# Moving side work to other steps in an attention and conv kernel: first chunks, fetches, reciprocals, last k and v, a band

## The chip, the cores and the metric

The kernel runs on one core of a Trainium2 chip. The metric is the device time of one execution in microseconds (us). TensorE (PE) multiplies, ScalarE (ACT) and VectorE (DVE) work elementwise, GpSimd (POOL) issues the accumulating DMAs and does small things, SyncE (SP) issues most of the other DMAs. Each engine works through its own instructions in order, and an instruction waits until what it needs is there.

## The reference

The input x is 4 images of 128 channels and 64 x 64 pixels, float32. Two layers follow each other. The first is attention with a residual:

```python
x_norm = _group_norm(x, norm_w, norm_b)              # 8 groups of 16 channels
qkv = jnp.einsum('oc,bchw->bohw', qkv_w, x_norm) + qkv_b[None, :, None, None]
q, k, v = jnp.split(qkv, 3, axis=1)                  # 4 heads of 32 channels, 4096 positions
attn = jax.nn.softmax(jnp.einsum('bhid,bhjd->bhij', q, k) * scale, axis=-1)
out = jnp.einsum('bhij,bhjd->bhid', attn, v)
return x + proj(out)
```

The second is a block of two 3x3 convolutions with quantized weights (3 bits), each followed by a batch norm over all four images, and a residual:

```python
out = jax.nn.relu(batchnorm(conv3x3(x, lsq_quantize(w1, alpha1))))
out = batchnorm(conv3x3(out, lsq_quantize(w2, alpha2)))
return jax.nn.relu(out + x)
```

## The kernel before

**Attention.** The queries of each image are cut into 8 blocks of 512 (`blocks`, 32 in all, numbered n; b is the image and qb the block in it). A block goes over the 4096 keys in 32 steps of 128, called kt. A step has two pairs of heads: `scores` (line 442) multiplies q and k for one pair into PSUM and ScalarE takes the exponential (`p`, line 444). `weights` (line 456) multiplies `p` with v into `acc`, in two halves of 256 queries each. The sum over keys is kept elementwise in `r` by VectorE (lines 469 and 471), except for the steps in `MOVED` = 4, 9, 14, 19, 24, 28, whose `p` tiles are summed into `rm` by accumulating DMAs of 1 MB each on GpSimd's queue (lines 464 and 466). `merge` (line 492) adds `rm` to `r` by another one at the start of the next block. There are 9 buffers for `p` tiles, 9 for k, 9 for v, 2 for q and 3 for x chunks.

**The order.** The order is written out by hand. The loop takes three pairs of scores, then three halves of weights, and so on, so TensorE goes in groups: 12 score matmuls, 24 value matmuls. After each half the function `side` emits what is due. `schedule(n, before)` makes this list for block n: `add(kt, f)` puts f after step kt, `at_half(p, f)` after half p, and `visit(i, first, second, evacuate)` puts matmuls of a projection at the end of the i-th group (`ends[i]`), both parts in one place if `split` is False, and the copy out of PSUM one half later. A place in this list is a place in each engine's order; it isn't a time.

**What is at its side.** After a block its result is finished during the next one: `sums` multiplies `r` by ones (`l`, line 488), `spread` stores the sums in another layout (`lq`, line 523), `invert` takes the reciprocals and stores them to DRAM (`rd`, line 529), `gather` reads them back spread over 128 partitions (`rc`, line 534), `weigh` multiplies (`av`, line 537), `residual` loads the x chunk, `project` and `store` end it (`po`, `y<-x`). `project_parts` gives the chunks: 512 columns of k, q or v, each 16 or 32 small matmuls (line 317) and copies on ScalarE and VectorE (lines 351, 352, 371); the chunks k and q go to DRAM (`kd`, `qd`) and come back by `load_k` and `load_q` in another layout. The norm of the next image is done by `late[b]`, of which entry 8 computes v's bias `bvn`. `pieces` are small steps of the quantization of the conv weights.

**The start.** The x chunks of image 0 are loaded, `keep_warm` issues matmuls that nobody reads, the statistics are taken (`mv`, `gm`), and the first chunks of k, q and v are projected before the first scores. The other chunks of image 0 lie in block 0, and the queries of blocks 2 to 7 in block 1.

**The conv.** A band is 18 rows of the padded image; `load_band` reads it from DRAM (line 582), `split_band` parts it in a high and a low half (`hi`, `lo`, lines 573 and 574), `conv` multiplies both (line 781). `layer` goes through the 16 bands and calls `prepare(m)` (here `first`) after band m. The first bands are loaded in the last attention block.

The loads and stores on SyncE's queue all stand in one order, and when one waits, those behind it wait too.

Of the kernel before, what the change touches and what calls it, by code (L numbers as in the profile page):

```python
# [78 lines left out]
def _fast_body(ctx, tc, x, norm_w, norm_b, qkv_wt, qkv_b, proj_wt, proj_b,  # L79
               w1, alpha1, gamma1, beta1, w2, alpha2, gamma2, beta2, out, cnt):  # L80
    nc = tc.nc
# [4 lines left out]
    NB = N // FB  # L86
# [53 lines left out]
    wqd = dram.tile([P, TAPS, P], F32, name="wqd")  # L140
# [80 lines left out]
    sums = att.enter_context(tc.tile_pool(name="sums", bufs=2))  # L221
# [84 lines left out]
    def keep_warm(count):  # L306

        t = psa.tile([P, FB], F32, name=f"idle{count}", tag="a")
        for _ in range(count):
            nc.tensor.matmul(t[:, 0:P], gavg, gavg, start=True, stop=True)  # L310
# [95 lines left out]
    def load_k(b, j):  # L406
        k = k_tile(b, j)
        for s in range(4):
            i, part = divmod(s, 2)
            src = kd[b, j][part].rearrange("(g i d) n -> i d g n", i=2, d=D)  # L410
            nc.sync.dma_start(out=f32(k)[s * D : (s + 1) * D, :, :], in_=src[i])
# [5 lines left out]
    def load_q(b, j):  # L417
        q = q_tile(b, j)
        src = qd[b, j].rearrange("s (g i d) n -> i g d s n", i=2, d=D)
        for s in range(4):  # L420
            for g in range(2):
                nc.sync.dma_start(out=f32(q)[s * D : (s + 1) * D, g, :, :], in_=src[s // 2, g])
# [161 lines left out]
    def split_band(b, g):  # L584
        ready[0, b, g] = split(raw[b, g], f"0_{b}_{g}")
# [5 lines left out]
        eng.dma_start(out=halves[j // 4][:, j % 4, :], in_=x_chunk(0, j))  # L591
    table = const.tile([P, 1], F32, name="table")
    nc.scalar.activation(table, mhalf, AF.Exp)
    keep_warm(26)
    st = small.tile([P, NB, 6], F32, name="st0", tag="st")
    for j in range(NB):
        nc.vector.bn_stats(st[:, j, :], halves[j // 4][:, j % 4, :])
# [14 lines left out]
    def load_kv(b, j):  # L612
        load_k(b, j)
        load_v(b, j)

    for what, j in (("k", 0), ("q", 0), ("k", 1), ("v", 0), ("k", 2), ("v", 1), ("k", 3), ("v", 2),
                    ("v", 3)):
        for f in first_chunk(j, what, True):
            f()
        if what == "q":  # L620
            five_v()
            six_v()
        if what == "v" and j < 3:
            load_k(0, j + 1)


# [3 lines left out]
    def fetch(b, j):  # L630
        xin[b, j] = load_x(b, j)

    def schedule(n, before):
        b, qb = blocks[n]
        todo = []
        ends = [p for p in range(2 * NK - 2) if (2 * n * NK + p) % 3 == 2]
        two = b + 1 < B and qb in ((3, 4, 5) if b == 0 else (2, 3))

        def at_half(p, f):
            todo.append((p, f))  # L640

        def add(kt, f):
            todo.append((2 * kt + 1, f))

        def visit(i, first, second, evacuate=None, split=True):
            at_half(ends[i], first)
            e = ends[i + 1 if split else i]
            at_half(e, second)  # L650
            if evacuate:
                at_half(e + 1, evacuate)
            return e

        if before:
            add(1, before["merge"])
            e = visit(5 if two else 4 if n == 1 else 6, lambda: before["sums"](0), lambda: before["sums"](1),
                      split=not two and n != 1)
            at_half(e + 2, before["spread"])
            at_half(e + 6, before["invert"])  # L660
            at_half(e + 8, before["gather"])
            at_half(e + 12, before["residual"])
            at_half(ends[18] - 4, before["weigh"])
            at_half(ends[18], before["project"])
            at_half(ends[18] + 2, before["store"])
        if n + 1 < len(blocks):
            add(24 if n == 0 else 14, lambda: load_q(*blocks[n + 1]))
        if n == 0:
            for i, what, j in ((0, "k", 4), (2, "k", 5), (4, "v", 4), (6, "k", 6), (8, "v", 5),
                               (10, "k", 7), (12, "q", 1), (14, "v", 6), (16, "v", 7)):  # L670
                visit(i, *first_chunk(j, what, False), split=False)
                if what == "k":
                    at_half(ends[i] + 5, lambda j=j: load_k(0, j))
        if n == 0:
            for j in (2, 3):
                add(25 + j, lambda j=j: fetch(0, j))
        if n == 1:
            for i, j in zip((0, 2, 8, 10, 12, 14), range(2, NB)):
                if j > 3:
                    at_half(ends[i - 3], lambda j=j: fetch(0, j))  # L680
                visit(i, *project_parts(0, j, lambda j=j: xin[0, j])["q"], split=False)
        qn = qb if b else qb - 1
        if b + 1 < B:
            if qn == 1:
                st = small.tile([P, NB, 6], F32, name=f"st{b + 1}", tag="st")
                for j in range(NB):
                    add(3 * j // 2, lambda j=j: fetch(b + 1, j))
                    add(3 * j // 2 + 3, lambda j=j: nc.vector.bn_stats(st[:, j, :], xin[b + 1, j]))
                late[b] = norm_parts(b + 1, st)
                add(15, late[b][0])  # L690
                for i in (0, 1):
                    at_half(ends[13 + 2 * i], late[b][1 + 2 * i])
                    at_half(ends[13 + 2 * i] + 3, late[b][2 + 2 * i])
            if qn == 2:
                at_half(ends[1], late[b][5])
                at_half(ends[1] + 1, late[b][6])
                at_half(ends[1] + 1, late[b][7])
                at_half(ends[1] + 4, late[b][8])
            if b == 0:
                chunks = {2: (), 3: (0, 1), 4: (2, 3), 5: (4, 5), 6: (6,), 7: (7,)}  # L700
            else:
                chunks = {1: (), 2: (0, 1), 3: (2, 3), 4: (4,), 5: (5,), 6: (6,), 7: (7,)}
            for i, j in enumerate(chunks.get(qb, ())):
                p = project_parts(b + 1, j, lambda j=j: xin[b + 1, j])
                if not two:
                    for what, i in dict(k=1, q=10, v=13).items():
                        visit(i, *p[what])
                    continue
                for what, e in (dict(k=2, q=7, v=9) if i == 0 else dict(k=11, q=13, v=15)).items():
                    visit(e, *p[what], split=False)  # L710
                if i == 1:
                    add(8, lambda j=j: fetch(b + 1, j))
            if qn > 0 and qb + 1 in chunks:
                add(22, lambda j=chunks[qb + 1][0]: fetch(b + 1, j))
            if qb == NB - 1:
                for j in range(NB - 1):
                    add(4 * j + 1, lambda j=j: load_kv(b + 1, j))
        if b > 0 and qb == 0:
            add(1, lambda: load_kv(b, NB - 1))


        if b == B - 1 and qb < NB - 1:
            for kt in (1, 10, 20):
                add(kt, lambda: next(pieces, None))
        elif 0 < b and qb == 0:
            for kt in (1, 10, 15, 20, 25) + ((29,) if b == 1 else ()):
                add(kt, lambda: next(pieces))
        if n == len(blocks) - 1:
            add(5, lambda: load_band(0, 0))
            add(13, lambda: split_band(0, 0))  # L730
            add(17, lambda: load_band(0, 1))
            add(24, lambda: split_band(0, 1))
            add(27, lambda: load_band(0, 2))
        return sorted(todo, key=lambda t: t[0])
# [58 lines left out]
    last["residual"]()  # L793
    conv(ready[0, 0, 0], early[0][:, 1, :], 1, wq[0])
    split_band(*bandlist[2])
    last["sums_at_once"]()
    conv(ready[0, 0, 1], early[1][:, 0, :], 0, wq[0])
    conv(ready[0, 0, 1], early[1][:, 1, :], 1, wq[0])
# [6 lines left out]
    cv = [mid.tile([P, N], F32, name=f"cv{b}") for b in range(B)]  # L805
    raw_w = mid.tile([P, TAPS, P], F32, name="raw_w")
    wq.append(mid.tile([P, TAPS, P], F32R, name="wq1"))
    nc.sync.dma_start(out=raw_w, in_=wqd)


    a_q, a_g, a_n = ([small.tile([P, 1], F32, name=f"{n}{i}") for i in range(2)]
# [50 lines left out]
    def count_bad():  # L862

        big = small.tile([P, 1], F32, name="big")
        nc.vector.tensor_reduce(big, worst, AX.X, ALU.max)
        bad = small.tile([P, 1], F32, name="bad")
        nc.vector.tensor_scalar(bad, big, LIMIT, None, ALU.is_gt)
        nbad = psa.tile([P, FB], F32, name="nbad", tag="a")
        nc.tensor.matmul(nbad[0:1, 0:1], bad, ones[:, 0:1], start=True, stop=True)
        nc.vector.tensor_copy(cnt, nbad[0:1, 0:1])  # L870

    def first(m):
        if m == 5:
            count_bad()
        if m == 6:
            nc.vector.tensor_copy(wq[1], raw_w)
        if m + 3 < len(bandlist):
            load_band(*bandlist[m + 3])
        if m + 2 < len(bandlist) and m > 0:
            split_band(*bandlist[m + 2])  # L880
# [527 lines left out]
```

## Time and profile before

| | |
|---|---|
| time, median of 3 runs | 2569.15 us (2565.08 to 2569.88) |
| span of the profiled execution | 2567.4 us |
| TensorE busy | 2515.2 us |
| VectorE busy | 2137.1 us |
| ScalarE busy | 2086.7 us |
| GpSimd busy | 282.9 us |
| DMA, mean | 157 GB/s |
| blocks of attention, from the first copy of `acc` to the last | 108.6 to 2250.8 us |
| granted TensorE clock, mean | 0.992 |

Busy times overlap, as the engines work at the same time. In the profile's rows a number such as L442 is the line of the kernel; `s<-q,k` is what it writes and reads, with buffer numbers left out. In a timeline a row has the start, the length, the engine, the line, the operation and its count, and in brackets the idle time ahead of it and what ended it. In the waits a row has the total, the number of times and the longest. SPq is SyncE's queue of DMA issues. PE counts as busy while a matmul is in it, so it says nothing about how well the array is filled.

### The profile page before, as it was taken

Reading aid. Unit: us, or ns where it says so; the run is one execution under the profiler, and the core shown is the slowest. Engines: PE = TensorE matmul, PEld = TensorE weight load, DVE = VectorE, ACT = ScalarE, POOL = GpSimd, SP = SyncE. Lnnn points to the kernel's source line nnn. Section 1 sums busy time; section 2 is a strip of 40 time slices with the busy share of each in tenths; the row PEclk is TensorE's granted clock in tenths of the full one; section 3 lists DMA queues with packets and bytes.
Section 4 is the critical chain, followed back from the end, with each engine's and each line's share of the span. In section 5 each row is a group of like instructions: output and inputs, shape, how many; then the busy total and the mean of one; then the engine's idle time right before and its main releaser. Section 6 shows DMA issues by size and latency. Waiting matters only on the chain.

```text
span 2567.4 us, 65010 instructions
## 1 busy us (share of the span) xinstructions
PE 2515.2 (98%) x28696; PEld 1504.3 (59%) x28696; DVE 2137.1 (83%) x1402; ACT 2086.7 (81%) x2278; POOL 282.9 (11%) x462
## 2 busy tenths in 40 slices
PE   8999999999999999999999999999999999999995
PEld 6555555555555555555555555555555555567774
DVE  5889888889988898889988988889999999954345
ACT  5889888998988899999988999989999999911224
POOL 2111111111011111110111111111000011000000
PEclk9999999999999999999999999999999999999997
DMA  6777667688766776797767667896666667645004
GB/s 179 179 187 164 171 176 180 158 202 188 176 151 174 169 167 155 167 222 172 169 167 175 154 154 165 194 202 149 148 137 143 145 147 149 143 87 162 1 1 165
DMA packets 148825, 403.85 MB, mean 157 GB/s; under 512 B 59416, under 2 KB 60184, under 8 KB 119992
## 3 DMA queue, kind: packets, MB, share of 16 engines
q0 software_dynamic: 45984, 280.92, 47.8%
q1 hardware_dynamic: 100680, 113.07, 17.3%
q10 hardware_dynamic: 1872, 5.64, 0.6%
q8 instruction: 227, 3.72, 0.6%
q14 instruction: 62, 0.51, 0.1%
HBM read 107.48 MB, written 56.42 MB: 64 GB/s over the span
## 4 chain that ended last, share of the span: by engine, by line
PE 85%; DMA 6%; issue 4%; DVE 3%; ACT 1%; SPq 0%; POOL 0%; ACTq 0%; POOLq 0%; DVEq 0%
PE s L442 38%; PE acc L456 34%; PE c L781 8%; DMA rm<-p 3%; DVE r L471 2%; PE pk L317 1%; PE l L488 1%; PE po L317 1%; PE pq L317 1%; PE pv L317 1%; DMA t<-y 1%; ACT p L444 1%; DMA rd<-rq 0%; ACT res L946 0%; DMA x<-in_x_dram 0%
## 5 line engine op out<-in xcount | busy, mean ns | idle before, releaser
L444 ACT ACTIVATE p<-s 128x1024 f32<-128x1024 f32 x2048 | 1949.6, 1032 | 216.0 <-PE s L442 161.4
L471 DVE TENSOR_TENSOR r<-r,p 128x2048 f32<-128x2048 f32 x768 | 1758.2, 2289 | 69.4 <-ACT p L444 18.7
L442 PE MATMUL s<-q,k 64*128 64x512 f32 x8192 | 1140.6, 409 | 6.7 <-ACT p L444 5.5
L456 PE MATMUL acc<-p,v 128*32 128x256 f32 x16384 | 1027.1, 383 | 1.0 <-DVE v L371 1.0
L442 PEld LDWEIGHTS s<-q,k 64*128 64x128 f32 x8192 | 715.1, 185 | 417.4 <-issue 167.7
L456 PEld LDWEIGHTS acc<-p,v 128*32 128x32 f32 x16384 | 462.6, 109 | 485.6 <-issue 249.2
L466 POOL DMA_DIRECT2D rm<-p x160 | 139.1, 870 | 848.0 <-ACT p L444 602.7
L848 ACT COPY cv<-c 128x512 f32<-128x512 f32 x60 | 35.2, 587 | 204.1 <-DVE st L847 204.1
L781 PE MATMUL c<-hi,wq 128*128 128x512 f32 x540 | 140.4, 404 | 3.8 <-DVE hi L573 2.5
L781 PE MATMUL c<-lo,wq 128*128 128x512 f32 x540 | 138.6, 401 | 0.0
L847 DVE BATCH_NORM_STATS2 st<-c 128x6 f32<-128x512 f32 x60 | 41.9, 699 | 103.1 <-PE c L781 82.8
L781 PEld LDWEIGHTS c<-hi,wq 128*128 128x128 f32 x540 | 102.2, 190 | 33.4 <-issue 5.0
L781 PEld LDWEIGHTS c<-lo,wq 128*128 128x128 f32 x540 | 101.6, 188 | 27.2
L352 DVE SCALAR_TENSOR_TENSOR kst<-pk,b,kst 128x512 fp32r<-128x512 f32 x32 | 24.0, 750 | 81.3 <-PE s L442 54.9
L469 DVE TENSOR_TENSOR r<-p,p 128x2048 f32<-128x2048 f32 x32 | 73.2, 2288 | 14.9 <-ACT p L444 14.9
L352 DVE SCALAR_TENSOR_TENSOR qst<-pq,b,qst 128x512 fp32r<-128x512 f32 x32 | 24.0, 751 | 71.9 <-PE s L442 59.7
L356 POOL DMA_DIRECT2D qd<-qst x31 | 23.1, 744 | 277.3 <-DVE qst L352 271.1
L492 POOL DMA_DIRECT2D r<-rm x31 | 26.2, 846 | 214.5 <-DMA rm<-p 100.1
L356 POOL DMA_DIRECT2D kd<-kst x28 | 20.8, 744 | 200.1 <-DVE kst L352 189.9
L488 PE MATMUL l<-r,ones 128*32 128x256 f32 (+1 forms) x504 | 37.7, 383 | 0.7 <-DMA r<-rm 0.7
L351 ACT ACTIVATE kst<-pk,b 128x512 fp32r<-128x512 f32 x32 | 22.3, 700 | 18.4 <-PE pk L317 18.4
L317 PE MATMUL pq<-x,wn 128*32 128x256 f32 x480 | 33.3, 379 | 3.9 <-DMA x<-in_x_dram 2.9
(149 smaller groups left out, 725.7 us busy)
## 6 DMA issues: line engine op xcount, KB each, us to landing
rm<-p POOLq DMA_DIRECT2D x192, 1024.0 KB, 7.6
q<-qd SPq DMA_DIRECT2D x248, 128.0 KB
r<-rm POOLq DMA_DIRECT2D x31, 1024.0 KB, 7.6
x<-in_x_dram SPq DMA_DIRECT2D x86, 256.0 KB
k<-kd SPq DMA_DIRECT2D x124, 128.0 KB
qd<-qst POOLq DMA_DIRECT2D x31, 512.0 KB, 7.5
kd<-kst POOLq DMA_DIRECT2D x28, 512.0 KB, 3.8
y<-x POOLq DMA_DIRECT2D x32, 256.0 KB, 7.1
```

What stands on the lines that cost most here:

```text
L317: nc.tensor.matmul(out[cs, :], w[:, cs], x, start=True, stop=True)
L352: nc.vector.scalar_tensor_tensor(lo, ps[what], bias, t[:, 0, :], ALU.add, ALU.subtract)
L356: (nc.sync if start else nc.gpsimd).dma_start(out=dst[b, j].rearrange("s p n -> p s n"), in_=t)
L442: nc.tensor.matmul(s[:, i, :], k[r, half, c0 : c0 + P], q[r, half, part, :], start=(part == 0), stop=(part == 1))
L444: nc.scalar.activation(pts[step][:, 2 * half : 2 * half + 2, :], s, AF.Exp, scale=SCALE)
L456: nc.tensor.matmul(acc[n][h * D : (h + 1) * D, cs], v[:, kt % KB, h * D : (h + 1) * D], pt[:, h, cs], start=(kt == 0 and half == 0), stop= ...
L466: nc.gpsimd.dma_start(out=msum[n], in_=pt, accum_op=ALU.add)
L469: nc.vector.tensor_tensor(rsum[n], pts[step - 1], pt, ALU.add)
L471: nc.vector.tensor_tensor(rsum[n], rsum[n], pt, ALU.add)
L488: nc.tensor.matmul(t["l"][h * D : (h + 1) * D, cs], ones, r[:, h, cs], start=first, stop=end)
L781: nc.tensor.matmul(ps.rearrange("p (r w) -> p r w", w=W), w[:, tap, :], part[:, r0 + kh : r0 + kh + RB, kw : kw + W], start=(n == 0), stop ...
L847: nc.vector.bn_stats(st[:, b * NB + c, :], ps[:, j, :])
```

## The change

The change moves work to other places in the order and takes nothing away, but for 12 more matmul instructions in `keep_warm`. It is meant to have inputs on hand earlier and to part things that come together.

- `keep_warm` at the start gets 32 rounds, before 26.
- Chunk k4 of image 0 is projected ahead of block 0; the others in block 0 move up by one place in the list, and with them their k loads; the first `load_q` comes at step 22, before 24.
- In block 1 the sums are at visit 5 (before 4), the chunks of q2 and q3 at 1 and 3 (before 0 and 2), and the x fetches two visits earlier.
- In every block `invert` comes 8 halves after the sums (before 6) and `gather` 15 (before 8), so behind `residual` (12, as before).
- `bvn` is computed two halves earlier, and the first chunk of k in a block with two chunks is at visit 3 (before 2).
- The last k and v tiles of an image are loaded at steps 9 and 16 of its first block (before both at 1), and `pieces` lie at slightly other steps.
- The fourth band of the first image is loaded ahead of the last block's sums (before: after the first band's conv, behind the load of the second conv's weights), and the conv weights `raw_w` after the third band.

```diff
-    keep_warm(26)
+    keep_warm(32)
...
     for what, j in (("k", 0), ("q", 0), ("k", 1), ("v", 0), ("k", 2), ("v", 1), ("k", 3), ("v", 2),
-                    ("v", 3)):
+                    ("k", 4), ("v", 3)):
...
-        if what == "v" and j < 3:
+        if what == "v":
             load_k(0, j + 1)
...
-            e = visit(5 if two else 4 if n == 1 else 6, lambda: before["sums"](0), lambda: before["sums"](1),
+            e = visit(5 if two or n == 1 else 6, lambda: before["sums"](0), lambda: before["sums"](1),
                       split=not two and n != 1)
             at_half(e + 2, before["spread"])
-            at_half(e + 6, before["invert"])
-            at_half(e + 8, before["gather"])
+            at_half(e + 8, before["invert"])
             at_half(e + 12, before["residual"])
+            at_half(e + 15, before["gather"])
...
-            add(24 if n == 0 else 14, lambda: load_q(*blocks[n + 1]))
+            add(22 if n == 0 else 14, lambda: load_q(*blocks[n + 1]))
         if n == 0:
-            for i, what, j in ((0, "k", 4), (2, "k", 5), (4, "v", 4), (6, "k", 6), (8, "v", 5),
-                               (10, "k", 7), (12, "q", 1), (14, "v", 6), (16, "v", 7)):
+            for i, what, j in ((0, "k", 5), (2, "v", 4), (4, "k", 6), (6, "v", 5), (8, "k", 7),
+                               (10, "q", 1), (12, "v", 6), (14, "v", 7)):
...
-            for i, j in zip((0, 2, 8, 10, 12, 14), range(2, NB)):
+            for i, j in zip((1, 3, 8, 10, 12, 14), range(2, NB)):
                 if j > 3:
-                    at_half(ends[i - 3], lambda j=j: fetch(0, j))
+                    at_half(ends[i - 5], lambda j=j: fetch(0, j))
...
-                at_half(ends[1] + 4, late[b][8])
+                at_half(ends[1] + 2, late[b][8])
...
-                for what, e in (dict(k=2, q=7, v=9) if i == 0 else dict(k=11, q=13, v=15)).items():
+                for what, e in (dict(k=3, q=7, v=9) if i == 0 else dict(k=11, q=13, v=15)).items():
...
-            add(1, lambda: load_kv(b, NB - 1))
+            add(9, lambda: load_k(b, NB - 1))
+            add(16, lambda: load_v(b, NB - 1))
...
-            for kt in (1, 10, 20):
+            for kt in (3, 11, 21):
...
-            for kt in (1, 10, 15, 20, 25) + ((29,) if b == 1 else ()):
+            for kt in (3, 12, 17, 22, 26) + ((29,) if b == 1 else ()):
...
     split_band(*bandlist[2])
+    load_band(*bandlist[3])
     last["sums_at_once"]()
...
-    nc.sync.dma_start(out=raw_w, in_=wqd)
...
+        if m == 2:
+            nc.sync.dma_start(out=raw_w, in_=wqd)
...
-        if m + 3 < len(bandlist):
+        if 0 < m < len(bandlist) - 3:
             load_band(*bandlist[m + 3])
```

## The prediction

> **What bounds the kernel now.** I read the page first (engines, slices, chain), then TensorE's waits, then the timeline around every wait, last the waits of SyncE's DMA queue.
>
> ```profile
> span 2567.4 us, 65010 instructions
> PE 2515.2 (98%) x28696; PEld 1504.3 (59%) x28696; DVE 2137.1 (83%) x1402; ACT 2086.7 (81%) x2278; POOL 282.9 (11%) x462
> PE 85%; DMA 6%; issue 4%; DVE 3%; ACT 1%; SPq 0%; POOL 0%; ACTq 0%; POOLq 0%; DVEq 0%
> ```
>
> TensorE sets the time: 98% of the span and 85% of the chain. No edit removes a matmul, so only TensorE's gaps and its slowed clock can be won. The gaps (TensorE's view of who waited for whom: total, times, longest):
>
> ```profile
> PE s L442 <- ACT p L444: 5.5, 10, 3.1
> PE pq L317 <- DMA x<-in_x_dram: 2.9, 2, 2.7
> PE gm L254 <- DVE mv L249: 2.8, 1, 2.8
> PE c L781 <- DVE hi L573: 2.5, 1, 2.5
> PE pq L317 <- ACT av L481: 1.1, 1, 1.1
> PE pk L317 <- DVE bvn L296: 1.0, 1, 1.0
> PE acc L456 <- DVE v L371: 1.0, 1, 1.0
> PE s L442 <- DMA q<-qst: 1.0, 1, 1.0
> PE l L488 <- DMA r<-rm: 0.7, 1, 0.7
> ```
>
> All are single events and each can be placed. The ruler is the distance between two 24-matmul value groups: 3.03 us plain, 3.89 with a projection chunk between (3.46 with half of one), almost without scatter over 683 groups. From the timeline at 135 to 151 us, a chunk, a plain group, then a stall of 6.77 = 3.89 + 2.88:
>
> ```profile
> 135.74 1.50 PE L456 MATMUL acc<-p,v 128*32 128x256 f32 x24
> 137.06 1.05 PE L317 MATMUL pq<-x,wn 128*32 128x256 f32 x16
> 139.63 1.50 PE L456 MATMUL acc<-p,v 128*32 128x256 f32 x24
> 142.66 1.50 PE L456 MATMUL acc<-p,v 128*32 128x256 f32 x24
> 146.84 1.07 PE L317 MATMUL pq<-x,wn 128*32 128x256 f32 x16 [2.67 <-DMA x<-in_x_dram]
> 149.43 1.50 PE L456 MATMUL acc<-p,v 128*32 128x256 f32 x24
> ```
>
> Three more rows, from the timelines at 1718 to 1732 us, 2238 to 2312 us and 0 to 45 us: ScalarE waiting for a `p` buffer that a 1 MB `rm<-p` move still reads; the fourth conv band arriving late; and the start, where 12 small matmuls take 2.91 us.
>
> ```profile
> 1727.88 4.69 ACT L444 ACTIVATE p<-s 128x1024 f32<-128x1024 f32 x5 [3.96 <-DMA rm<-p]
> ...
> 2282.52 3.71 PE L781 MATMUL c<-hi,wq 128*128 128x512 f32 x9 [2.51 <-DVE hi L573]
> ...
> 14.61 2.91 PE L310 MATMUL idle<-gavg 128*128 128x128 f32 x12
> ```
>
> Last, SyncE's own waits, the second and the sixth row: it stands 6.2 us per block (192.6 / 31) at the store of the reciprocals, with everything behind it held, and then again for that store to land.
>
> ```profile
> SPq L529 <- DVE worst L531: 192.6, 31, 8.6
> ...
> SPq L534 <- DMA rd<-rq: 58.6, 16, 6.6
> ```
>
> **What the Trainium skill says.** "TensorE: Matmul & The Clock Gate", section "What's actually happening": the array falls to half clock after an idle window of about 3.4 us and comes back after a busy one. The trace agrees: nine conv matmuls take 3.71 us after the 2.51 us gap and 2.32 us later on; the clock is 0.89 in the first 30 us, and 0.97 in the two 64 us windows with the gaps at 1728 and 2282 us. A gap of 2.5 us or more is thus paid again. "DMA: Bandwidth & Descriptors", "Issuing engines are not separate DMA queues": all issuers share the same 16 engines. The trace agrees in kind: a move of 7.6 us (median in the table of issues) takes 12.5 us when SyncE's loads pile up around it. Same page, "Two DMAs through the same engine are not ordered": a dependent DMA needs its issuer to wait for the first; that is the 58.6 us row above.
>
> **The change part by part.**
>
> *Start, `keep_warm` 26 to 32.* Its 52 matmul instructions take 7.74 us, so 12 more end near 11.4 us, ahead of the statistics at 12.45 us (wait 2.82 us). The gap falls to about 1.1 us. If the clock then holds, the small matmuls from 12.45 to 18.09 us run at about half their time (6 idle ones 1.63 us, 12 idle ones 2.91 us, both in front of needed ones), and the first `pk` takes 1.05 in place of 1.53 us. Following the chain mean, variance, `wn`, `pk` with those halves moves the first `kst` from 19.70 to about 17.3 us: at most 2.4 us, at least 0. I take 1.8.
>
> *Chunk k4 into the prologue.* It leaves block 0, where a chunk costs 3.89 - 3.03 = 0.86 us, and adds 1.05 us of TensorE before the first scores. Those wait anyway for `q<-qst` (1.00 us, at 30.0), so it is hidden: 0.86 won. Its 0.75 us of VectorE lies ahead of v3's copy, first needed at kt 12.
>
> *Block 0's other chunks, one visit earlier.* v6 was visited at group 14 and its copy on VectorE came after two 2.29 us additions, so the value group at 86.6 us took 4.10: 1.07 us. Now it has two visits more. I take 1.0.
>
> *Block 1.* q2 at visit 1 no longer asks for the PSUM bank that `av`'s copy frees (group at 106.7 us: 5.15 - 3.89 = 1.26); take 1.2. The sums at visit 5 come a group after the wait for `r<-rm` (121.8 us: 4.84 - 3.89 = 0.95); take 0.9. The x fetches are issued two visits earlier (2.88, and 0.40 at 159.4 us); take 3.1. Here a wait is added: with three `x` buffers, x7's fetch now stands behind the residual's and needs x5's buffer, so SyncE waits there for q5's matmuls, with `load_q` (8.4 us of issues) and the gather behind it. By about 150 us both are out, and their users come at 167 us and later: nothing.
>
> *Reciprocals and gather later in all blocks; last k and v apart.* SyncE passes `load_q` and one k load before it stands at the store. In blocks 7, 15 and 23, where the next batch's k and v go out, this pulls the end of the pile forward by up to those 6 us; v7, 256 KB, falls behind the spread. The stalls it meets, as groups: at 607 to 618 us 0.20 + 1.31, at 1161 to 1170 us 1.82 + 0.21, at 1723 to 1735 us 4.27 + 0.71 (the last with half clock), sum 8.5 us. I take three quarters, 6.4. The gather's place is 7 half-steps later, 7 us, but as SyncE waits less ahead of it, its time moves little; its user `weigh` stood 14 to 31 us behind it.
>
> *Statistics of v.* `bvn` at +2 rather than +4 and k at visit 3: at 743 to 753 us two group lengths take 9.69 where 2 x 3.03 + 0.86 + 0.97 (gb and gw, from blocks with short waits) is 7.89. I take 1.3 of the 1.8, since the 0.35 us wait of `gw` for `b` stays.
>
> *Fourth band, conv weights.* The band is loaded before the last sums, not behind `raw_w`, which SyncE issues at 2274.79 only after `y<-x` has landed. TensorE's 2.51 us and the slow nine (3.71 - 2.32 = 1.39) go: 3.9. `raw_w` is used four bands of 8.6 us later; hidden. The `pieces`' new steps cost nothing: VectorE is 83% busy and the groups of batch 3 stay at 3.03.
>
> Sum: 1.8 + 0.86 + 1.0 + 1.2 + 0.9 + 3.1 + 6.4 + 1.3 + 3.9 = 20.5 us. I take off 1.5, one new stall of the size of those seen, since the order of SyncE's issues changes in every block: 19.0. 2569.15 - 19.0 = 2550.
>
> **The rivals.**
>
> *The pile stays.* For it: SyncE runs ahead; it waits 1148 us in all for the spread's sums, so a load placed at kt 9, still ahead of the spread, may leave when it did before, and only v7 moves. Against: the 6 us at the store. Then 2 of the 6.4 remain: 14.6, 2555.
>
> *All of it goes*, the clock holding in the start: 2.4 + 0.86 + 1.07 + 1.26 + 0.95 + 3.28 + 8.5 + 1.8 + 3.9 = 24.0, nothing new: 2545.
>
> *New waits eat most of it.* For it: three x buffers, nine `p` buffers of which k4's staging holds one more, the band's 576 KB beside the last 1 MB move, and in the last block the gather behind a band load. Against: each has some us of room. Twelve us back: 2562.
>
> *The gather comes too late: slower.* The shortest way from gather to `weigh` is 14.2 us (1959.0 to 1973.2). Less 7 us of place and about 7 us to land, nothing is left; if `weigh` holds VectorE by 2 us in half of the 31 blocks, and TensorE's projection with it, that is 32 us against 14: 2587. Against it: the gather's issue follows the landing of `rd`, which the longer distance no longer makes SyncE await.
>
> **How the numbers follow.** Main case 0.52, pile stays 0.24, all goes 0.13, new waits 0.07, slower 0.04. The time is the main case's, 2550. The range 2543 to 2560 holds the first three (0.89) with about 2 us for the measurement, whose three runs lie 4.8 us apart. 0.2% is 5.1 us: faster means under 2564. Main, pile, all and most of the new waits are faster: 0.93; within 0.2%: 0.03, what is left of the new waits; slower 0.04.
>
> **What would show it.** In the changed profile: TensorE's waits for `x<-in_x_dram`, `av`, `hi` and `v` gone; the wait for `mv` near 1 us and the clock of the first 30 us above 0.95; ScalarE's waits for `rm<-p` (8.8 us before) under 3; SyncE's wait at L529 well under 192.6 us; one chunk fewer in block 0. Wrong would be: a new row of 2 us or more in TensorE's waits, `po` waiting for `av` in many blocks (the gather), or the `rm<-p` waits as before.

## The result and the profile after

The changed kernel takes 2547.1 us (median of 6 runs, 2546.47 to 2548.74), the kernel before 2567.74 us beside it (6 runs, 2562.96 to 2569.88): ratio 0.9923, 95% interval 0.991 to 0.9936. The page of the changed kernel, the same three lines:

```profile
span 2547.0 us, 65043 instructions
PE 2509.0 (99%) x28708; PEld 1503.6 (59%) x28708; DVE 2137.2 (84%) x1402; ACT 2087.4 (82%) x2278; POOL 281.6 (11%) x461
PE 92%; issue 3%; DMA 2%; DVE 1%; ACT 1%; ACTq 0%; POOL 0%; SPq 0%; POOLq 0%; DVEq 0%
```

The span is 20.4 us shorter. The busy times of the other engines are within 1.3 us of those before; TensorE's is 6.2 us less, and its idle time falls by the other 14.2. Three stretches of half clock in the trace of before (6.8 us from 12.2 us on, 3.4 us from 1729.2 and 3.4 us from 2282.1 us on) are gone. TensorE's share of the chain goes from 85% to 92% as that of DMA falls from 6% to 2%. TensorE's waits of the changed kernel (total, times, longest):

```profile
PE po L317 <- DVE av L537: 2.2, 2, 1.8
PE idle L310 <- POOL mhalf L110: 1.9, 1, 1.9
PE c L782 <- issue: 1.3, 1, 1.3
PE gm L254 <- DVE mv L249: 1.0, 1, 1.0
PE s L442 <- ACT p L444: 0.9, 5, 0.2
PE pv L317 <- DVE v L371: 0.9, 1, 0.9
PE s L442 <- DVE v L371: 0.7, 1, 0.7
PE gw L291 <- DVE b L286: 0.7, 1, 0.7
```

The rows for `x`, `hi`, `av`'s copy on ScalarE, `bvn` and `r<-rm` are gone. The largest was shorter before:

```profile
PE po L317 <- DVE av L537: 0.9, 2, 0.5
```

Now `po` waits 1.8 us for `av` in one block, number 23. The four places of the timeline that were shown of before, in the changed kernel (block 1, without the rows of the scores; the start of image 3's first block; the fourth conv band's first `hi` row; the idle matmuls of the start):

```profile
136.17 1.50 PE L456 MATMUL acc<-p,v 128*32 128x256 f32 x24
137.49 1.05 PE L317 MATMUL pq<-x,wn 128*32 128x256 f32 x16
140.04 1.50 PE L456 MATMUL acc<-p,v 128*32 128x256 f32 x24
143.05 1.50 PE L456 MATMUL acc<-p,v 128*32 128x256 f32 x24
144.37 1.05 PE L317 MATMUL pq<-x,wn 128*32 128x256 f32 x16
...
1713.13 4.69 ACT L444 ACTIVATE p<-s 128x1024 f32<-128x1024 f32 x5 [0.48 <-DMA rm<-p]
...
2263.12 2.31 PE L782 MATMUL c<-hi,wq 128*128 128x512 f32 x9
...
14.14 1.60 PE L310 MATMUL idle<-gavg 128*128 128x128 f32 x12
```

The chunk at 144.37 us follows its group without a wait. ScalarE waits 0.48 us where it waited 3.96, the band's matmuls wait for nothing and run at full clock, and twelve idle matmuls take 1.60 us in place of 2.91.

To see where the 20.4 us come from, cut the span at the first value group and at the copies of `acc` that end each block (L481). All are differences of start times in the traces:

| stretch | before, us | after, us | difference |
|---|---|---|---|
| start to first value group | 34.3 | 31.9 | -2.4 |
| block 0 from there | 74.3 | 72.5 | -1.8 |
| block 1 | 76.55 | 70.94 | -5.6 |
| the six blocks at the borders of images: 7, 8, 15, 16, 23, 24 | 414.90 | 409.89 | -5.0 |
| block 10 | 73.16 | 72.22 | -0.9 |
| block 31 | 63.34 | 62.59 | -0.75 |
| the other 22 blocks | 1514.26 | 1514.05 | -0.2 |
| after the last block | 316.6 | 312.9 | -3.7 |

The 22 blocks in which nothing had waited did not move. This is the ruler for the experiments too: it repeats to some tenths of a us where nothing was touched (1514.0 to 1514.6 us in all runs), but for the start, which varies with the arrival of x. The stretches that the change touches scatter more. In the runs that leave them as changed, block 0 takes 72.4 to 73.5 us, block 10 takes 71.9 to 72.6 and the six border blocks together take 407.9 to 409.9.

SyncE's waits, the row of the store (now in two parts, as the last releaser differs) and that of the gather:

```profile
SPq L529 <- DVE worst L531: 94.5, 20, 9.0
SPq L529 <- DVE worst L530: 87.9, 8, 12.9
SPq L534 <- DMA rd<-rq: 45.8, 14, 5.9
```

Together the store's waits are 182 us after 192.6 before: they hardly fell. SyncE has more issues ahead of the store now, but the reciprocals that the store waits for are made later too. In block 18 the store leaves 13.6 us after the spread, 8.6 before, and SyncE stands there for 13.0 us in place of 8.0. In the last blocks of images 0, 1 and 2 alone it stands for 0.1, 0.1 and 1.5 us in place of 2.5, 4.1 and 6.8.

### The profile page after: what moved, and what is told of

Its sections match the earlier page's. It is cut to its first block, busy times and chain, and to the rows that moved or that the text cites. A ratio compares the mean times of both kernels' runs of the same rounds, so it can differ in the third digit from the quotient of the medians.

```text
span 2547.0 us, 65043 instructions
## 1 busy us (share of the span) xinstructions
PE 2509.0 (99%) x28708; PEld 1503.6 (59%) x28708; DVE 2137.2 (84%) x1402; ACT 2087.4 (82%) x2278; POOL 281.6 (11%) x461
## 4 chain that ended last, share of the span: by engine, by line
PE 92%; issue 3%; DMA 2%; DVE 1%; ACT 1%; ACTq 0%; POOL 0%; SPq 0%; POOLq 0%; DVEq 0%
PE s L442 41%; PE acc L456 36%; PE c L782 9%; DMA rm<-p 2%; PE l L488 1%; PE pq L317 1%; PE pk L317 1%; PE po L317 1%; PE pv L317 1%; DVE r L471 1%; ACT p L444 0%; ACT res L949 0%; DMA xh<-in_x_dram 0%; PE c_last L782 0%; DVE res L948 0%
## 5 line engine op out<-in xcount | busy, mean ns | idle before, releaser
L466 POOL DMA_DIRECT2D rm<-p x160 | 139.5, 872 | 800.4 <-ACT p L444 535.5
L782 PEld LDWEIGHTS c<-hi,wq 128*128 128x128 f32 x540 | 101.2, 188 | 30.3 <-issue 2.1
L469 DVE TENSOR_TENSOR r<-p,p 128x2048 f32<-128x2048 f32 x32 | 73.2, 2288 | 12.1 <-ACT p L444 11.1
L464 POOL DMA_DIRECT2D rm<-p x32 | 17.8, 557 | 176.8 <-ACT p L444 93.4
```

Of the source, the lines that this page charges most:

```text
L466: nc.gpsimd.dma_start(out=msum[n], in_=pt, accum_op=ALU.add)
L469: nc.vector.tensor_tensor(rsum[n], pts[step - 1], pt, ALU.add)
L782: nc.tensor.matmul(ps.rearrange("p (r w) -> p r w", w=W), w[:, tap, :], part[:, r0 + kh : r0 + kh + RB, kw : kw + W], start=(n == 0), stop ...
```

## The experiments

All are edits of the changed kernel, timed against the kernel before on the same chip (4 runs of each, 7 of before). First the control, the changed kernel itself.

> The changed kernel itself, as a control on the same chip: 2546.5 to 2548.7, the stall of block 23 and the 2.3 us at the borders as in its first profile if they belong to the order, otherwise moved or gone.

Measured: 2548.41 us (2547.5 to 2549.48), ratio 0.9918 (0.9902 to 0.9935). The six border blocks take 409.4 us, block 23 has its 1.8 us wait of `po` again. It belongs to the order.

### What mends the borders: the reciprocals' places or those of k7 and v7?

Both places of the reciprocals undone:

```diff
-            at_half(e + 8, before["invert"])
+            at_half(e + 6, before["invert"])
+            at_half(e + 8, before["gather"])
             at_half(e + 12, before["residual"])
-            at_half(e + 15, before["gather"])
```

> The changed kernel with invert and gather back at 6 and 8 halves, gather ahead of residual; k7 and v7 stay at steps 9 and 16. Measured at the three borders of images (blocks 7/8, 15/16, 23/24): the excess of the value groups over 3.03 us was 9.3 us before and is 2.3 us after. Theory (SyncE standing at the store of the reciprocals caused the pile): the excess comes back to 6 us or more, the 2.05 us stall of block 23 (po behind a late gather) goes, total 2549 to 2551. Rival (only the place of k7 and v7 counts): the excess stays near 2.3, block 23's stall goes, total 2545.

Measured: 2553.83 us (2552.03 to 2555.18), ratio 0.9942 (0.9925 to 0.9958). Border blocks 415.3 us: all of their gain is lost, as the theory had it, and the total lies above its 2549 to 2551. Block 23's stall is gone, block 31 is back at 63.35. The clock falls to half at 1719.7 us for 3.4 us, as it did before the change at this border.

The last k and v undone:

```diff
-            add(9, lambda: load_k(b, NB - 1))
-            add(16, lambda: load_v(b, NB - 1))
+            add(1, lambda: load_kv(b, NB - 1))
```

> The changed kernel with k7 and v7 both back at step 1 of an image's first block. Theory (the store's place): the excess at the borders grows by at most 2 us, to 2.3 to 4.3, total 2547 to 2549, with block 23's stall still there. Rival (place of k7 and v7): the excess comes back to 6 us or more, total 2551 to 2554.

Measured: 2547.15 us (2545.42 to 2547.98), ratio 0.9916 (0.99 to 0.9933). Border blocks 409.0 us, within the scatter of the runs that leave them as changed. This edit brings nothing that can be seen once the reciprocals have moved.

Both undone:

> The changed kernel with both of these undone. Both theories: excess at the borders about 9, block 23's stall gone, total 2552 to 2554. If it stays under 5, neither of the two moves made it, but the steps of the weight pieces or the different time of everything did.

Measured: 2551.96 us (2551.22 to 2556.08), ratio 0.9935 (0.9919 to 0.9952). Border blocks 417.9 us, 2.7 above the run with the reciprocals alone undone. Whether k7 and v7 at their new places help under the old order of the reciprocals is not shown: this trace is of the slowest of the four runs, its clock is at half for 6.8 us in block 24 where the other's is for 3.4, and the two medians lie the other way round. The `pieces` keep their new steps here, and nothing of the border blocks' gain is left: their steps alone do not make it.

### The gather or the store?

In the last block of an image, the gather put ahead of the residual's fetch and of k4 and v4; the store stays at 8:

```diff
+            if qb == NB - 1:
+                at_half(e + 12, before["gather"])
             at_half(e + 12, before["residual"])
-            at_half(e + 15, before["gather"])
+            if qb < NB - 1:
+                at_half(e + 15, before["gather"])
```

> The changed kernel, but in the last block of an image (where the next image's k and v are loaded) the gather stands ahead of the residual's fetch and of k4 and v4, at 12 halves; elsewhere as changed. Theory (the gather lands 14 us late in block 23 since it stands behind 2 MB of loads in SyncE's queue): VectorE's wait for rc (4.1 us) and po's wait of 1.8 us go, the value group of 5.94 us becomes 3.89, total 2545. Rival (the landing is late because all DMA engines are busy, whoever stands ahead): the wait stays over 1 us and the total at 2547.

Measured: 2550.81 us (2547.14 to 2551.49), ratio 0.9927 (0.991 to 0.9944). The stall of block 23 is gone as expected, and the block takes 68.0 us in place of 70.0. But the five other border blocks take 344.9 us where they took 339.9. The expected 2 us were won and 5 lost.

Now the store alone back at 6 halves, the gather left at 15:

```diff
-            at_half(e + 8, before["invert"])
+            at_half(e + 6, before["invert"])
```

> The changed kernel with the reciprocals and their store back at 6 halves, the gather left at 15. In the last blocks of images 0, 1 and 2 SyncE stood idle ahead of the store for 2.5, 4.1 and 6.8 us before the change and for 0, 0 and 1.5 us after it, with the q and k loads behind; the six blocks at the borders (7, 8, 15, 16, 23, 24) took 414.9 us before, 409.9 after, 415.3 with both places undone and 412.9 with the gather alone ahead of the fetches. Theory (any standing of SyncE ahead of these loads costs, at the store as at the gather): the idle time comes back and the six blocks take 413 us or more, total 2551 or more. Rival (only the gather's place counts): the six blocks take 410, total 2548.

Measured: 2554.14 us (2553.62 to 2555.3), ratio 0.9949 (0.9933 to 0.9966); six border blocks 416.15 us. Both numbers are those of the theory, and yet in five of the six blocks its cause is absent: without block 23 they take 340.0 us, as in the changed kernel, and block 23 alone takes 76.2. ScalarE's waits for `rm<-p` in this run, then with both places undone:

```profile
ACT p L444 <- DMA rm<-p: 3.3, 3, 1.9
```

```profile
ACT p L444 <- DMA rm<-p: 9.6, 5, 4.0
```

The run with both places undone differs from this one in the gather's place alone. So the late store does not free the `p` buffers; the late gather does. This wait is 8.8 us before the change and 9.6, 12.7 and 9.6 us in the three runs above with an early gather in the border blocks (both places undone, all four undone, gather first). It is 4.4 and 2.7 us in the changed kernel's two profiles, 2.2 with k7 and v7 undone and 3.3 here. A fourth run with an early gather, the version with k7 behind the spread below, has 5.6.

The store's place counts for another thing. In this run the gather of block 23 is issued 4 us later after the spread than in the changed kernel (25.3 us in place of 21.1, since SyncE stands 6.8 us at the store with k3, v3 and q behind it), and lands too late for `weigh`. TensorE's timeline there, from the last value group ahead of it:

```profile
1691.96 1.50 PE L456 MATMUL acc<-p,v 128*32 128x256 f32 x24
1698.92 1.94 PE L317 MATMUL po<-av,wp 128*32 128x512 f32 x8 [5.45 <-DVE av L537]
1700.78 2.93 PE L442 MATMUL s<-q,k 64*128 64x512 f32 x12
1703.64 1.94 PE L456 MATMUL acc<-p,v 128*32 128x256 f32 x24
```

A wait of 5.45 us for `av`, and then twelve score matmuls take 2.93 us in place of 1.66: the trace has half clock for 6.8 us from 1697.8 us. The two new places are a pair. The late gather relieves the moves, and the later store lets k3 and v3 out first, so that the late gather isn't later still.

A part of what the early gather does to the moves can be seen on SyncE's queue in block 7. With both places undone:

```profile
565.50 0.54 SPq L534 DMA_DIRECT2D rc<-rd  x1
566.09 0.47 SPq L235 DMA_DIRECT2D x<-in_x_dram  x1
566.67 2.85 SPq L411 DMA_DIRECT2D k<-kd  x4
569.63 0.36 SPq L415 DMA_DIRECT2D v<-vd  x1
570.36 7.01 SPq L411 DMA_DIRECT2D k<-kd  x4
577.47 0.41 SPq L415 DMA_DIRECT2D v<-vd  x1
```

With the store alone undone, the gather behind k4 and v4:

```profile
565.12 0.37 SPq L235 DMA_DIRECT2D x<-in_x_dram  x1
565.71 3.18 SPq L411 DMA_DIRECT2D k<-kd  x4
569.00 0.36 SPq L415 DMA_DIRECT2D v<-vd  x1
569.40 0.54 SPq L534 DMA_DIRECT2D rc<-rd  x1
570.06 3.64 SPq L411 DMA_DIRECT2D k<-kd  x4
573.80 1.20 SPq L415 DMA_DIRECT2D v<-vd  x1
```

Up to 570 us the two are level, and the store stands alike in both. With the gather in front, the four issues of k5 take 7.01 us in place of 3.64, and v5 leaves 3.7 us later. In the same block the moves after it start at 31.6 and 42.7 us after the spread with the late gather, and at 32.9 and 43.7 with the early one. Why a gather of 256 KB, ahead of k4, slows k5's issue by this much no run here shows.

### A version with k7 behind the spread

The edit of the gather above, and

```diff
-            add(9, lambda: load_k(b, NB - 1))
+            add(13, lambda: load_k(b, NB - 1))
```

> The changed kernel with the gather first in an image's last block, and besides k7 at step 13 of the next, which is behind the spread in SyncE's order, where before it stood ahead and could leave at once. Theory: block 23's 2.05 us and most of the 2.3 us at the borders go: 2543 to 2544. Rival (k7 behind the spread delays q and the reciprocals of that block): 2545 or more.

Measured: 2545.85 us (2545.32 to 2548.45), ratio 0.9908 (0.9892 to 0.9925), border blocks 408.6 us. The 2543 to 2544 us of the theory were not reached; the rival's number, 2545 or more, was. It lies 2.6 us under the control of the same chip, but the ranges overlap, as do the intervals: whether it beats the changed kernel is not settled. Beside the run with the gather first alone, blocks 7, 15 and 24 fall from 69.2, 74.0 and 70.0 us to 68.0, 72.7 and 68.3; the five border blocks without 23 take 340.7 us in place of 344.9, and the wait for `rm<-p` is 5.6 us in place of 9.6. So the late gather is not the only cure: with the gather in front, taking k7 out of the pile of loads mends nearly as much. And k7 at step 9 had not waited for its step. It stood ahead of the spread in SyncE's order and left when SyncE got there, still in block 7; at 13 it stands behind the spread of block 8. The gather first alone, then this version:

```profile
587.67 3.14 SPq L411 DMA_DIRECT2D k<-kd  x4
```

```profile
619.16 0.56 SPq L523 DMA_DIRECT2D lq<-ls  x1
...
621.14 3.95 SPq L411 DMA_DIRECT2D k<-kd  x4
```

### The other edits, each undone alone

`keep_warm(26)`:

> The changed kernel with keep_warm(26) as before. Theory (the idle 2.8 us ahead of the statistics drops the clock to half for 6.8 us): the first value group starts 2.4 us later, at 34.3, small idle matmuls take 0.24 us each again, total 2549.5. Rival (the start is bound by the q loads, as the wait of 1.00 us for q<-qst said): under 0.5 us later, total 2547.

Measured: 2549.81 us (2549.2 to 2553.51), ratio 0.9933 (0.9916 to 0.995). The first value group starts at 34.5 us, with half clock from 12.3 us for 6.8 us. TensorE's timeline of this run:

```profile
12.51 0.58 PE L254 MATMUL gm<-mv,gavg 128*128 128x1 f32 x2 [2.88 <-DVE mv L249]
12.96 1.63 PE L310 MATMUL idle<-gavg 128*128 128x128 f32 x6
14.38 0.42 PE L263 MATMUL gv<-dv,gavg 128*128 128x1 f32 x2
14.66 2.91 PE L310 MATMUL idle<-gavg 128*128 128x128 f32 x12
17.36 0.43 PE L281 MATMUL gb<-gc,wqkv 128*128 128x1 f32 x2
```

The 2.88 us of idle time and the half-speed rows are those of before (2.82 us). No run with 32 rounds has half clock in the start; they wait for `mv` for 2.4 us at most, in the control.

The fourth band and `raw_w` as before the change (the diff above, reversed):

> The changed kernel with the fourth band and the conv weights issued as before. Theory: TensorE waits 2.5 us for hi again and the next nine matmuls take 3.7 us at half clock; total 2550.8 (+3.7). Rival (the fourth band's time is given back later in the conv, as VectorE's splits follow one another): the wait is there but the total is within 1 us of the changed kernel.

Measured: 2550.93 us (2550.33 to 2552.28), ratio 0.9934 (0.9918 to 0.9951). After the last block 316.8 us, in place of 312.9. The wait is back, and the clock is at half from 2265.4 us for 3.4 us:

```profile
2264.19 3.27 PE L782 MATMUL c<-hi,wq 128*128 128x512 f32 x9 [2.43 <-DVE hi L573]
2267.26 2.98 PE L782 MATMUL c<-lo,wq 128*128 128x512 f32 x9
```

Block 1 as before, with the gather at its new place:

```diff
-            e = visit(5 if two or n == 1 else 6, lambda: before["sums"](0), lambda: before["sums"](1),
+            e = visit(5 if two else 4 if n == 1 else 6, lambda: before["sums"](0), lambda: before["sums"](1),
...
-            for i, j in zip((1, 3, 8, 10, 12, 14), range(2, NB)):
+            for i, j in zip((0, 2, 8, 10, 12, 14), range(2, NB)):
...
-                    at_half(ends[i - 5], lambda j=j: fetch(0, j))
+                    at_half(ends[i - 3], lambda j=j: fetch(0, j))
```

> The changed kernel with block 1 as before: sums at visit 4, chunks at 0 and 2, x fetches at ends[i-3]. The gather stays at 15 halves. Theory: block 1 takes 76 us again, of it 1.26 for av, 0.95 for r<-rm, and up to 3.3 for x; total 2552 (+5.5). Rival (the x wait came from the old gather standing ahead of the fetch, and is mended by the gather's new place alone): the x wait stays away and only 2.2 us come back, total 2549.

Measured: 2552.61 us (2549.92 to 2552.92), ratio 0.9937 (0.992 to 0.9953); block 1 takes 76.6 us. TensorE waits 2.1 us for `x`, 1.1 for `av` and 0.7 for `r<-rm`. The rival falls: with the old fetches, x is late under the new gather as well.

k4, the other chunks of block 0 and the first `load_q` as before (the diff above, reversed):

> The changed kernel with k4 back in block 0 and the other chunks and load_q as before. Theory: 0.86 us for the chunk and 1.07 for v6's late copy, total 2549.0 (+1.9). Rival (k4 in the prologue delays the first scores by the 1.05 us that it takes, as the start is shorter now): the first scores come up to 0.7 us earlier here, and the total is 2548.2 or less.

Measured: 2548.05 us (2547.62 to 2548.45), ratio 0.9922 (0.9905 to 0.9938). Block 0 from the first value group takes 74.3 us in place of 72.5, with a 4.10 us group before v6's copy, but the first value group comes at 30.8 us. In other runs with 32 rounds and k4 in front it comes at 30.3 to 32.9, so the start can't be told apart from its scatter. The total, under the rival's 2548.2, doesn't settle it either. In sum the edit is worth somewhere between nothing and 1.8 us.

`bvn` and the first k as before:

```diff
-                at_half(ends[1] + 2, late[b][8])
+                at_half(ends[1] + 4, late[b][8])
...
-                for what, e in (dict(k=3, q=7, v=9) if i == 0 else dict(k=11, q=13, v=15)).items():
+                for what, e in (dict(k=2, q=7, v=9) if i == 0 else dict(k=11, q=13, v=15)).items():
```

> The changed kernel with bvn at +4 and the first k at visit 2 as before. Theory: the two value groups of block 10 take 9.7 us again in place of 8.2 with the k chunk counted, blocks 3 and 18 change by under 0.3; total 2548.0 (+0.9). Rival (VectorE's idle time ahead of bvn, which the change brings, costs as much elsewhere): total 2547 or less.

Measured: 2550.77 us (2548.24 to 2552.39), ratio 0.993 (0.9914 to 0.9947). Block 10 takes 73.2 us, 0.6 to 1.4 more than in the runs that leave it as changed; blocks 3 and 18 stay at 74.6. Which of the two edits does it is open, as they were undone together. The median lies 2.4 us above the control, which the profile doesn't explain: it is of the fastest of the four runs (2548.24 us).

## Why the prediction held, and where its reasons did not

The forecast was 2550 us in a range of 2543 to 2560; 2547.1 was measured. The forecast gain of 19.0 us stands against 20.6. Most terms of the sum were right in cause and size. In the largest, that of the reciprocals and the gather, only the size was right, and that is luck.

- **The bound, and what there was to win.** Right. TensorE's single waits and the half clock behind some of them were the whole of it. The blocks without a wait did not move.
- **Start.** Taken as 1.8 us of at most 2.4, measured 2.4 in the profile. The clock is the cause of a part: it falls to half in both traces with 26 rounds and in none of the twelve with 32. The size is partly chance: in those twelve the first value group comes at 30.3 to 32.9 us.
- **k4 and v6.** Taken as 0.86 + 1.0, measured 1.8 within block 0. That k4's 1.05 us are hidden in the start is not shown, as the start's scatter is larger.
- **Block 1.** Taken as 1.2 + 0.9 + 3.1 = 5.2, measured 5.6; undone it comes back as 76.6 us. The added wait of x7's fetch cost nothing that can be seen.
- **Reciprocals, gather, last k and v.** Taken as 6.4 less 1.5 for one new stall, measured 5.0 net: the five blocks without block 23 lose 7.1 us, block 23 gains 2.1. The size is right, the cause is not. "SyncE passes `load_q` and one k load before it stands at the store" is what happened at the borders; that this pulls the pile forward is what failed. With the store early and the gather late, the five blocks are as fast, and in block 7 k5 leaves 18.9 us after the spread there and 19.0 in the changed kernel. What freed the `p` buffers was the gather's place behind k4 and v4, of which I had said that its time moves little. And "SyncE's wait at L529 well under 192.6 us" did not come true (182 us), since the store itself moved later with the reciprocals.
- **v7 behind the spread.** Worth nothing that can be seen (409.0 us with k7 and v7 as before, 409.9 and 409.4 with the change). The rival that the pile stays was right in that k7 leaves as it did, 34.3 us after the spread of block 7 before and 33.4 after, and wrong in that this would keep the stalls.
- **The gather too late.** The rival that ends slower was real in one block out of 31: `rc`, issued at 1679.66 us, held VectorE's `weigh` until 1693.98, 14.3 us later, behind k4, v4 and eight q loads in the same queue. It cost the 2.1 us of block 23.
- **`bvn`.** Taken as 1.3, measured 0.9: the wait of `gw` for `b`, expected to stay at 0.35, is 0.66 us.
- **Fourth band.** Taken as 3.9, measured 3.7 and 3.9.
- **The signs.** Most came: the waits for `x` and `hi` are gone, `mv` is waited for 1.0 us and the clock of the first 30 us is 1.00. ScalarE's wait for `rm<-p` was to fall under 3 us: it is 4.4 in the first profile and 2.7 in the control. And a row of 2 us or more, which was to speak against the forecast if it was new, is there: `po`'s, 2.2 us, grown from 0.9.
- **The clock.** The fall behind the 2.51 us gap was read as agreeing with a window of about 3.4 us that has to be idle. The same trace keeps full clock behind the longer wait of 2.67 us for `x` in block 1; that no loss was added there was right, but no reason was given for it. The last section has one.
- **The long moves.** The prediction lays a move of 12.5 us, where the median is 7.6, to SyncE's loads that pile up around it. But moves of 11.9 to 12.9 us stand in each of the last seven blocks of that trace too, where no k or v of another image is loaded. So the pile of k and v is not what sets them apart.
- **Not seen:** 0.75 us in block 31. It is back (63.35 us) with the reciprocals' places undone, but not with k7 and v7 undone besides (62.83), so its cause is open.

## What to carry to other kernels

Where one engine is busy nearly all the time, list its single waits, measure each as the excess over an undisturbed group, and see in the trace's clock whether the matmuls behind it ran at half; here the sum of such terms forecast the gain within 2 us. A place in an in-order queue is no time: a load moved to a later step leaves as early as before unless something that waits stands in front of it, so ask what lies ahead of it and what it will lie ahead of. When two moves are made together, look at the blocks one by one: a total can match a theory whose cause is absent.

## What the runs showed of the hardware

**The clock.** The Trainium skill's page "TensorE: Matmul & The Clock Gate" ("What's actually happening") has a clock that halves after an idle window of about 3.4 us, and a window that runs free of the kernel. The traces agree on the second point. In each of the 14, every change of the granted clock lies a whole multiple of 3.413 us after the first one, and the first lies anywhere from 4.75 to 8.03 us, though the first matmul starts at 1.9 us in all of them. On the first point they differ: the clock also fell after windows that were not idle. Cut the span into windows of 3.413 us that begin at the first change:

| trace, window in us | TensorE's wait | TensorE busy in the window | clock after it |
|---|---|---|---|
| before, 1725.74 to 1729.15 | 3.07 for `p` | 0.34 us | half |
| before, 8.83 to 12.24 | 2.82 for `mv` | 0.80 us | half |
| block 1 undone, 153.00 to 156.41 | 2.12 for `x` | 1.29 us | half |
| before, 2278.70 to 2282.11 | 2.51 for `hi` | 1.31 us | half |
| both places undone, 1716.28 to 1719.69 | the end of 3.12 for `p` | 1.49 us | half |
| control, 1692.39 to 1695.80 | 1.77 for `av` | 1.64 us | full |
| control, 9.61 to 13.03 and the next | 2.44 for `mv`, cut in two | 1.73 and 2.66 us | full |
| before, 141.95 to 145.37 and the next | 2.67 for `x`, cut in two | 2.21 and 1.95 us | full |

In all 14 traces the clock fell 23 times, the kernel's end included, each time after a window with at most 1.49 us of busy TensorE. It did not fall after any of the other 10297 windows at full clock, each with 1.64 us or more. So what decides in these traces is not the length of a wait but how little TensorE has done within one window, and that changes from run to run with the place of the windows. After a fall the clock stayed at half for one window or two (3.4 or 6.8 us), and for longer at the kernel's end. A wait with a fall behind it costs more than its length: the 2.51 us for `hi` made the nine matmuls behind it 1.39 us longer, and the 5.45 us in block 23 made the block 8.2 us longer than with no stall (76.2 and 68.0 us).
